# Attention kernel on one Trainium2 core: the sums of the last two batches inverted in other ways, and bias loads, projections and last products in another order

## The chip, the core and the metric

The kernel runs on one core of a Trainium2 chip. The metric is the time of one execution on the device in microseconds (us), as the median of several runs. The core has TensorE (PE in the profile; its weight loads are PEld), VectorE (DVE), ScalarE (ACT), GpSimd (POOL) and SyncE (SP, which here only issues DMAs). All data is 32-bit float.

## What is computed

For 32 images of 256 channels and 32 x 32 positions (S = 1024):

```python
h = group_norm(x, G=32)                       # 8 channels to a group, no scale or shift
q = einsum('oc,bcs->bos', q_w, h) + q_b
k, v = split(einsum('oc,bcs->bos', kv_w, h) + kv_b)
# 8 heads of 32 channels; position s sees positions before it alone
scores = where(strictly_lower, q @ k.T / sqrt(32), -10000)
attn = where(strictly_lower, softmax(scores), 0)
out = x + attn @ v
```

## The kernel before

**Tiles.** An image is a batch of the kernel. Its 8 heads form two groups `g` of four heads (4 x 32 = 128 channels, the partitions). The queries are cut into two halves `hf` of 512. So a batch has four output tiles, n = 2g + hf, each 128 channels x 512 positions.

**Visits.** Scores stand transposed: keys on the partitions (blocks of 128), queries on the free axis. A batch is N = 12 visits, six to a group. In each visit `scores` makes one full piece (4 heads x 512 columns, tile `e`) and one half piece (4 x 256, tile `eh`): score matmuls (L269) into six PSUM banks `sT`, exponentials on ACT (L321 for `e`, L319 for `eh`), and, where a block lies on the diagonal, a mask on POOL (L283). Only blocks that a query can see are made; there is no running maximum. Two of the half piece's matmuls (`first`) stand ahead of the full piece's.

**Loop.** The main loop runs i over all B x N visits and once more. In pass i it issues the scores of visit i, then the functions listed for i under `at`, then `values` of visit i-1, then those under `after`. The order on PE, ACT, DVE and POOL is the order of issue. `when(i, f)` puts a function in such a list; PROJECT, PREPARE, SUMS and FINISH hold the places in visits from the batch's first.

**Values and sums.** `values` multiplies the exponentials with v on TensorE into `acc` (L343). VectorE adds the same exponentials elementwise into the first piece of the tile, `total` (L348), so that the sum over keys in the end needs one reduction over 128 partitions. `num` is ACT's copy of `acc` (L351).

**From total to inverse: three ways.**

- Batches up to B-3 fold: a DMA on POOL's queue adds partitions 64 to 127 of `total` onto 0 to 63, another 32 to 63 onto 0 to 31 (`fold`, L362); SP's DMA stacks the four tiles' 32 rows (`stack`, L368); VectorE turns them in 32 x 32 blocks (L375) and reduces (L376) (`sum_folded`). Then `check_sums` (L434, L435), a reciprocal (L440), a turn (L446), a DMA to DRAM and one back that repeats each head's row over 32 partitions, into `rb` (L453).
- Batch B-2 and the first two tiles of B-1: `sums` multiplies `total` with a matrix of ones on TensorE (`pd`, eight matmuls as counted in the profile, L383), ACT copies the result (`den`, L416), SP writes the rows to DRAM, `gather` reads them back in another shape, and then check, reciprocal and the way over DRAM as above.
- The last two tiles of B-1: `pd` holds the sum on all 32 partitions of a head already, so VectorE takes the reciprocal of the whole 128 x 512 tile in place (`check_here`, `invert_here`, L493). For n = 3 the last three pieces before the final visit, and the final visit's two, are not added by VectorE: `sum_piece` sums them on TensorE.

**Finish.** `finish` is two operations on VectorE (product with the inverse L466; plus v's bias and x L467), a copy of column 0 for tiles with hf = 0 (L469) and a store. `finish_aside` does it with two on POOL (L477, L478) and one on ACT (L479). At the end a count of sums outside a safe range (`outside`) is read by a branch; with the inputs given it goes past the safe version.

**Start.** SP loads x of batch 0 and the weights; ACT's queue loads the three biases. `norm_channels` takes mean and variance per channel on VectorE, two small matmuls (`pm`, `pv`) average over groups, `turn_weights` turns the weights on TensorE, `keep_busy` fills with matmuls on the unit matrix. `projections` gives the 12 units of a batch (8 for q and k, 4 for v) in the order in which they are placed; for batch 0 the first ones run before visit 0.

Of the kernel before, what the change touches and what calls it, by code (L numbers as in the profile page):

```python
# [9 lines left out]
F32 = mybir.dt.float32  # L10
# [21 lines left out]
def tile_norm_attention_residual(  # L32
# [55 lines left out]
    in_range = const.tile([P, ROW + 1], F32, name="in_range")  # L88
# [8 lines left out]
    def unshifted():  # L97
# [24 lines left out]
        def load_weights():  # L122
            for n, w in enumerate((q_w, kv_w[0:C], kv_w[C : 2 * C])):
                live["wn", n] = epool.tile([P, 4, HALFBANK], F32, tag="eh", bufs=4, name=f"wn_{n}")[:, :NG, :C]
                nc.sync.dma_start(out=live["wn", n], in_=w.rearrange("(o p) c -> p o c", p=P))
            nc.scalar.dma_start(out=qk_bias[:, 0, :], in_=q_b.rearrange("(g p) -> p g", p=P))
            nc.scalar.dma_start(out=qk_bias[:, 1, :], in_=kv_b[0:C].rearrange("(g p) -> p g", p=P))
            nc.scalar.dma_start(out=v_bias_col, in_=kv_b[C : 2 * C].rearrange("(g p) -> p g", p=P))
# [112 lines left out]
        def projections(b):  # L241

            qk = [[lambda g=g, hf=hf, n=n: project_qk(b, g, n, hf) for n in range(2)] for g in range(NG) for hf in range(NH)]
            v = [lambda n=n: project_v(b, n) for n in range(NB // 2)]
            return qk[0] + qk[1][:1] + v[:2] + qk[1][1:] + qk[2] + v[2:] + qk[3]
# [29 lines left out]
        def mask(pc, e):  # L275
# [3 lines left out]
            if k < hf * BPH:  # L279
                return  # L280
            n = len(blocks)
            diagonal = e[:, :, : n * P].rearrange("p j (n q) -> p j n q", q=P)
            nc.gpsimd.affine_select(  # L283
                out=diagonal, in_=diagonal, pattern=[[0, 4], [0, n], [1, P]],
                compare_op=ALU.is_gt, fill=0.0, base=0, channel_multiplier=-1,
            )
            if k == 0:
                nc.gpsimd.memset(e[0:1, :, 0:1], 1.0)

        def scores(b, full, half):  # L290
# [8 lines left out]
            first = [scores_of((b, half), short[:, j % 2, 1, :], j) for j in (2, 3)]  # L299


            for n in range(len(full[4])):
                for j in range(4):
                    scores_of((b, full), pairs[j // 2][:, j % 2, :], j, n)

# [22 lines left out]
            mask(full, e)  # L328
# [3 lines left out]
        def values(b, pc, summed=True):  # L332
            g, hf, k, part, blocks = pc
            first, last = k == 0, k == hf * BPH + (1 if hf == 0 else 2)
            e = live.pop(("e", b, pc)) if summed else live["e", b, pc]
# [3 lines left out]
            acc, total = live["acc"], live["sum", b, g, hf]  # L339
            for kb, cols, of in blocks:  # L340
# [6 lines left out]
                if not first and summed:  # L347
                    nc.vector.tensor_add(total[:, :, of], total[:, :, of], e[:, :, cols])  # L348
            if last:
# [38 lines left out]
        def sum_piece(b, pc, start=False, stop=False):  # L388

            if start:  # L390
                live["pd", b] = misc(f"pd_{b}")
            e = live.pop(("e", b, pc))
            for kb, cols, of in pc[4]:
                sum_keys(live["pd", b], e, cols, of, start, stop)

        def sum_total(b):
            sum_keys(
                live["pd", b], live["sum", b, NG - 1, NH - 1], slice(0, HALF), slice(0, HALF), False, False
            )

        def sums(b, g, hf):

            n = NH * g + hf
            den = small.tile([P, HALF], F32, tag="den", name=f"den_{b}_{n}")
            if (b, n) == (B - 1, 3):
                pd = live["pd", b]
            else:
                pd = misc(f"pd_{b}_{n}")
                sum_keys(pd, live.pop(("sum", b, g, hf)), slice(0, HALF), slice(0, HALF))
            if b == B - 1 and n >= 2:  # L410

                most = small.tile([P, 1], F32, tag="most", name=f"most_{n}")
                nc.scalar.activation(den, pd, AF.Identity, accum_out=most)
                live["most", n], live["den", n] = most, pd if n == 3 else den
                return
            nc.scalar.copy(den, pd)  # L416
            if n == 0:
                live["sums", b] = dram.tile([4, 4, HALF], F32, tag="sums", name=f"sums_{b}")
            nc.sync.dma_start(out=live["sums", b][n], in_=den[::HD, :])

        def spread_rows(t):
            return t.rearrange("n j (r c) -> (n j r) c", c=ROW)

        def gather(b, ns):

            if ns.start == 0:
                live["rows", b] = small.tile([P, ROW], F32, tag="rows", name=f"rows_{b}")
            part = slice(ns.start * HD, ns.stop * HD)
            nc.sync.dma_start(out=live["rows", b][part], in_=spread_rows(live["sums", b])[part])

        def check_sums(b, ns):
            part = slice(ns.start * HD, ns.stop * HD)
            rows, ok = live["rows", b][part], in_range[part, :ROW]
# [3 lines left out]
        def invert(b, ns):  # L437
            part = slice(ns.start * HD, ns.stop * HD)
            inv = small.tile([P, ROW], F32, tag="inv", name=f"inv_{b}_{ns.start}")
            nc.vector.reciprocal(inv[part], live["rows", b][part])  # L440
            live["inv", b] = dram.tile([4, 4, HALF], F32, tag="inv", name=f"inverses_{b}_{ns.start}")
            if b >= B - 2:
                nc.sync.dma_start(out=spread_rows(live["inv", b])[part], in_=inv[part])
            else:
                turned = small.tile([P, ROW], F32, tag="inv_turned", name=f"inv_turned_{b}")
                nc.vector.transpose(turned, inv)  # L446
                for n in ns:
                    nc.sync.dma_start(
                        out=live["inv", b][n].rearrange("(a j) (m c) -> (j m) a c", a=2, c=HD),
                        in_=turned[n * HD : (n + 1) * HD].rearrange("p (a c) -> p a c", a=2),  # L450
                    )
            for n in ns:
                nc.sync.dma_start(  # L453
                    out=inverses(b, n),
                    in_=live["inv", b][n].unsqueeze(1).broadcast_to([4, HD, HALF]),
                )

        def inverses(b, n):
            live["rb", b, n] = work.tile([P, HALF], F32, tag="rb", bufs=4, name=f"rb_{b}_{n}")
            return live["rb", b, n]  # L460

# [10 lines left out]
        def finish_aside(b, n, within=slice(0, HALF)):  # L472

            g, hf = divmod(n, NH)
            cols = slice(hf * HALF + within.start, hf * HALF + within.stop)
            num, rb, xt = live["num", b, n], live["rb", b, n][:, within], live["x", b]
            nc.gpsimd.tensor_tensor(rb, num[:, within], rb, ALU.mult)  # L477
# [6 lines left out]
        def check_here(n, ok):  # L484

            least = small.tile([P, 1], F32, tag="least", name=f"least_{n}")
            junk = small.tile([P, HALF], F32, tag="den", name=f"junk_{n}")
            nc.vector.tensor_scalar(junk, live["den", n], SUM_MIN, 1.0, ALU.is_ge, ALU.min, accum_out=least)
            nc.vector.scalar_tensor_tensor(ok, live["most", n], SUM_MAX, least, ALU.is_le, ALU.mult)

        def invert_here(b, n, within):
            rb = live["rb", b, n] if within.start else inverses(b, n)
# [303 lines left out]
```

## Time and profile before

| what | value |
|---|---|
| median of 4 runs | 1836.52 us (1834.83 to 1837.79) |
| profiled execution | 1836.38 us, span 1834.7 us |
| PE busy | 1814.5 us (99%) |
| DVE busy | 1650.2 us (90%) |
| ACT busy | 1481.3 us (81%) |
| POOL busy | 796.2 us (43%) |
| mean granted TensorE clock | 0.996 |

The span runs from the first to the last instruction of the profiled execution; its own time has 1.7 us around it. A row of a timeline gives the start, the length, the engine, the line, the operation, out<-in, shapes, a count, and in brackets how long the engine was idle before it and what ended that. Rows of one line behind each other are merged, so a length can hold several instructions. A row of stretches gives its bounds and length, then busy time by engine (PE, PEld, DVE, ACT, POOL, with counts), the granted clock, the DMA engines' busy share and GB/s.

### The profile page before, as it was taken

How to read it: one execution, taken by the hardware profiler on the slowest of the kernel's cores; microseconds unless marked ns; L12 is line 12 of the kernel's file. 1: busy time of each engine (PE TensorE's matmuls, PEld its weight loads, DVE VectorE, ACT ScalarE, POOL GpSimd, SP SyncE). 2: the span in 40 equal slices, each digit the busy share in tenths (PEclk: the TensorE clock that was granted, in tenths of full speed). 3: DMA queues.
4: the chain of work that ended last, by engine and by line, in shares of the span. 5: the costliest groups of instructions: out<-in, count | busy, mean ns of one | idle time of the engine just before them, and what ended most of it. 6: DMA issues, size and time to landing. Idle time of an engine off the chain costs nothing.

```text
span 1834.7 us, 53874 instructions
## 1 busy us (share of the span) xinstructions
PE 1814.5 (99%) x23200; PEld 925.4 (50%) x23200; DVE 1650.2 (90%) x1747; ACT 1481.3 (81%) x1871; POOL 796.2 (43%) x772
## 2 busy tenths in 40 slices
PE   8999999999999999999999999999999999999997
PEld 5455555555554555554545545555555455455443
DVE  3789999999999999999999999999999999999878
ACT  5888878888788888788887788887888877888775
POOL 1444534435434445444354344454453443444413
PEclk9999999999999999999999999999999999999998
DMA  3447676666766676766666656767667666667412
GB/s 122 70 84 137 138 152 114 127 135 138 145 131 118 134 139 135 152 114 126 136 140 142 133 119 133 140 134 151 116 124 139 137 143 134 120 133 138 87 51 84
DMA packets 77518, 231.46 MB, mean 126 GB/s; under 512 B 20288, under 2 KB 21312, under 8 KB 61912
## 3 DMA queue, kind: packets, MB, share of 16 engines
q0 software_dynamic: 15360, 94.39, 37.3%
q1 hardware_dynamic: 61096, 133.54, 24.1%
q8 instruction: 184, 3.01, 0.7%
q14 instruction: 62, 0.51, 0.1%
q10 hardware_dynamic: 816, 0.00, 0.0%
HBM read 67.42 MB, written 34.64 MB: 56 GB/s over the span
## 4 chain that ended last, share of the span: by engine, by line
PE 94%; DVE 3%; DMA 1%; ACT 1%; issue 0%; SPq 0%; DVEq 0%; ACTq 0%
PE sT L269 30%; PE acc L343 26%; PE pp L156 25%; PE ppv L156 13%; DVE e L348 1%; DMA folded<-e 1%; DVE rb L493 0%; DVE rb L466 0%; DVE rb L467 0%; DMA x<-in_x_dram 0%; ACT e L321 0%; PE pv L156 0%; DMA inverses<-inv_turned 0%; ACT eh L319 0%; PE pd L383 0%
## 5 line engine op out<-in xcount | busy, mean ns | idle before, releaser
L321 ACT ACTIVATE e<-sT 128x1024 f32<-128x1024 f32 x768 | 745.8, 1025 | 273.7 <-PE sT L269 204.7
L348 DVE TENSOR_TENSOR e<-e,e 128x1536 f32<-128x1536 f32 x381 | 638.5, 1676 | 20.3 <-POOL e L283 2.7
L348 DVE TENSOR_TENSOR e<-e,eh 128x1024 f32<-128x1024 f32 x381 | 523.6, 1388 | 132.8 <-PE acc L343 114.5
L283 POOL TENSOR_SCALAR_AFFINE_SELECT e<-e 128x512 f32<-128x512 f32 (+1 forms) x256 | 378.8, 1480 | 592.2 <-ACT e L321 572.1
L269 PE MATMUL sT<-q,k 32*128 32x256 f32 (+3 forms) x7168 | 606.8, 458 | 0.8 <-ACT k L223 0.8
L269 PEld LDWEIGHTS sT<-q,k 32*128 32x128 f32 x7168 | 443.6, 184 | 157.4 <-ACT eh L319 64.4
L156 PE MATMUL pp<-xn,wT 128*32 128x512 f32 x4096 | 492.3, 598 | 0.2 <-ACT den L416 0.2
L343 PE MATMUL acc<-e,v 128*32 128x512 f32 (+2 forms) x4096 | 400.7, 486 | 0.0
L319 ACT ACTIVATE eh<-sT 128x1024 f32<-128x1024 f32 x384 | 397.6, 1035 | 0.0
L362 POOL DMA_DIRECT2D e<-e x240 | 196.6, 825 | 376.6 <-DMA e<-e 286.0
L156 PE MATMUL ppv<-wT,xn 128*32 128x256 f32 x4096 | 247.3, 382 | 0.0
L343 PEld LDWEIGHTS acc<-e,v 128*32 128x32 f32 x4096 | 132.5, 110 | 223.4 <-issue 192.1
L343 PE MATMUL acc<-eh,v 128*32 128x256 f32 x3072 | 224.4, 379 | 0.0
L156 PEld LDWEIGHTS pp<-xn,wT 128*32 128x32 f32 x4096 | 107.0, 109 | 220.1 <-issue 204.3
L343 PEld LDWEIGHTS acc<-eh,v 128*32 128x32 f32 x3072 | 98.4, 110 | 165.0 <-issue 152.9
L156 PEld LDWEIGHTS ppv<-wT,xn 128*32 128x32 f32 x4096 | 120.2, 109 | 102.6 <-issue 29.5
L283 POOL TENSOR_SCALAR_AFFINE_SELECT eh<-eh 128x512 f32<-128x512 f32 x128 | 165.7, 1294 | 0.2
L209 ACT ACTIVATE xn<-x,shift,rstd 128x512 f32<-128x512 f32 x124 | 103.3, 833 | 0.0
L467 DVE SCALAR_TENSOR_TENSOR rb<-rb,v_bias_col,x 128x512 f32<-128x512 f32 x126 | 95.8, 760 | 4.5
L223 ACT ACTIVATE q<-pp,qk_bias 128x512 f32<-128x512 f32 x128 | 91.2, 712 | 1.9 <-PE pp L156 1.9
L223 ACT ACTIVATE k<-pp,qk_bias 128x512 f32<-128x512 f32 x128 | 89.8, 702 | 2.2 <-PE pm L156 1.1
L466 DVE TENSOR_TENSOR rb<-num,rb 128x512 f32<-128x512 f32 x126 | 88.0, 699 | 0.1
(69 smaller groups left out, 669.4 us busy)
## 6 DMA issues: line engine op xcount, KB each, us to landing
e<-e POOLq DMA_DIRECT2D x120, 512.0 KB, 6.3
x<-in_x_dram SPq DMA_DIRECT2D x64, 512.0 KB
out_dram<-rb SPq DMA_DIRECT2D x127, 256.0 KB
rb<-inverses SPq DMA_DIRECT2D x126, 256.0 KB
e<-e POOLq DMA_DIRECT2D x120, 256.0 KB, 4.9
folded<-e SPq DMA_DIRECT2D x120, 256.0 KB
inverses<-inv_turned SPq DMA_DIRECT2D x120, 8.0 KB
wn<-in_L_conv_kv_w_dram SPq DMA_DIRECT2D x2, 256.0 KB
```

The costliest lines, as they stand in the source:

```text
L156: nc.tensor.matmul(out[part], lhsT=lhsT[:, part], rhs=rhs, start=start, stop=stop, skip_group_check=True)
L209: nc.scalar.activation(xn, xt, AF.Identity, bias=live["shift", b][:, g : g + 1], scale=rstd)
L223: nc.scalar.activation(live[key][:, cols], pp, AF.Identity, bias=qk_bias[:, n, g : g + 1], scale=(SCALE, 1.0)[n],)
L269: return nc.tensor.matmul(pair[:, cols], lhsT=live["k", b, g][rows, kb * P : (kb + 1) * P], rhs=live["q", b, g][rows, hf * HALF + of.start ...
L283: nc.gpsimd.affine_select(out=diagonal, in_=diagonal, pattern=[[0, 4], [0, n], [1, P]], compare_op=ALU.is_gt, fill=0.0, base=0, channel_mu ...
L319: exp = nc.scalar.activation(eh.rearrange("p (n bank) q -> p bank n q", n=2), short, AF.Exp)
L321: nc.scalar.activation(e[:, 2 * a : 2 * a + 2, :], pairs[a], AF.Exp)
L343: nc.tensor.matmul(acc[HD * j : HD * (j + 1), of], lhsT=live["v", b][:, kb, h * HD : (h + 1) * HD], rhs=e[:, j, cols], start=first, stop=l ...
L348: nc.vector.tensor_add(total[:, :, of], total[:, :, of], e[:, :, cols])
L362: nc.gpsimd.dma_start(out=total[:rows], in_=total[rows : 2 * rows], accum_op=ALU.add)
L466: nc.vector.tensor_mul(rb, num[:, within], rb)
L467: nc.vector.scalar_tensor_tensor(rb, rb, v_bias_col[:, g : g + 1], xt[:, g, cols], ALU.add, ALU.add)
```

## The change

1. Batch B-2 is folded like the others. Its inverses are made in visit 8 of the last batch (`invert`), tiles 0 and 1 are finished on VectorE in visits 10 and 11, tiles 2 and 3 by `finish_aside` in the closing pass.
2. Each tile of the last batch is summed by `pd` alone and inverted by `invert_here`: VectorE turns the 128 x 512 `den` in 32 x 32 blocks, takes one column of each block (16 columns) for the check and the reciprocal, and turns a repeated reading of them back into the 128 x 512 `rb`. No DRAM is used. Tiles 0 and 1 are finished within the batch; tile 3 is inverted in halves of 256 straight from PSUM, and its `num` stays in `acc`.
3. VectorE adds every piece but those of the final visit; then the sum of tile 3's `total` is made on TensorE behind visit 10's values, and the final visit's pieces are summed ahead of their values.
4. In the final visit the `first` matmuls stand behind the full piece's first block, and the full piece is masked in two pairs of heads.
5. The bias loads go from ACT's queue to SP's, behind the weights; the scaling of q's bias goes behind the first half of batch 0's normalisation.
6. In every batch the first unit of v's projection comes ahead of the third of q and k; for batch 0 it runs before visit 0. The last piece of `norm_apply` comes one visit later.

The core of the diff:

```diff
-            nc.scalar.dma_start(out=qk_bias[:, 0, :], in_=q_b.rearrange("(g p) -> p g", p=P))
+            nc.sync.dma_start(out=qk_bias[:, 0, :], in_=q_b.rearrange("(g p) -> p g", p=P))
...
-            return qk[0] + qk[1][:1] + v[:2] + qk[1][1:] + qk[2] + v[2:] + qk[3]
+            return qk[0] + v[:1] + qk[1][:1] + v[1:2] + qk[1][1:] + qk[2] + v[2:] + qk[3]
...
-            first = [scores_of((b, half), short[:, j % 2, 1, :], j) for j in (2, 3)]
+            last = b == B - 1 and full[:2] == (NG - 1, NH - 1) and half[2] == NB - 2
+            first = [] if last else [scores_of((b, half), short[:, j % 2, 1, :], j) for j in (2, 3)]
...
+                first = first or [scores_of((b, half), short[:, j % 2, 1, :], j) for j in (2, 3)]
...
-            mask(full, e)
+            for heads in (range(2), range(2, 4)) if last else (range(4),):
+                mask(full, e, slice(heads.start, heads.stop))
...
-            if last:
+            if last and (b, g, hf) == (B - 1, NG - 1, NH - 1):
+                live["num", b, NH * g + hf] = acc
+            elif last:
...
+        def sums(b, n):
+            pd = misc(f"pd_{b}_{n}")
+            sum_keys(pd, live.pop(("sum", b, *divmod(n, NH))), slice(0, HALF), slice(0, HALF), True, n < 3)
+            if n == 3:
+                live["den", n] = pd
             else:
+                live["den", n] = small.tile([P, HALF], F32, tag="den", name=f"den_{b}_{n}")
+                nc.scalar.copy(live["den", n], pd)
...
+        def invert_here(b, n, within=slice(0, HALF)):
+            if within.start == 0:
+                inverses(b, n)
+            k = (within.stop - within.start) // HD
+            turned = small.tile([P, HALF], F32, tag="den", name=f"turned_{b}_{n}_{within.start}")[:, : k * HD]
+            nc.vector.transpose(turned, live["den", n][:, within])
+            rows = turned.rearrange("p (k r) -> p k r", r=HD)[:, :, 0]
+            check_sums(rows)
+            inv = small.tile([P, ROW], F32, tag="inv", name=f"inv_{b}_{n}_{within.start}")[:, :k]
+            nc.vector.reciprocal(inv, rows)
+            nc.vector.transpose(
+                live["rb", b, n][:, within].rearrange("p (k r) -> p k r", r=HD),
+                inv.unsqueeze(2).broadcast_to([P, k, HD]),
+            )
...
         def end_last(b):
+            both = [slice(c * HALFBANK, (c + 1) * HALFBANK) for c in range(2)]
+            for part in both:
+                invert_here(b, 3, part)
             worst = const.tile([P, 1], F32, name="worst")
             nc.vector.tensor_reduce(worst, in_range, AX.X, ALU.min)
-            check_here(3, ok)
-            invert_here(b, 3, both[0])
+            pc = misc("pc")
+            nc.tensor.matmul(pc[0:1, 0:1], lhsT=worst, rhs=ones, start=True, stop=True)
+            finish(b, 3, both[1])
+            finish(b, 2)
             outside = const.tile([1, 1], I32, name="outside")
             nc.vector.tensor_scalar(outside, pc[0:1, 0:1], -1.0, float(P), ALU.mult, ALU.add)
-            finish_aside(b, 3, both[0])
-            invert_here(b, 3, both[1])
-            finish(b, 3, both[1])
+            finish(b, 3, both[0])
...
-        PREPARE = (-16, -15, -9, -9, -8, -8, -7, -6, -5, -4)
+        PREPARE = (-16, -15, -9, -9, -8, -8, -7, -6, -5, -3)
...
+                    when(first + N + 8, lambda b=b: invert(b))
...
+                    for n in every[:2]:
+                        when(first + N + 10 + n, lambda b=b, n=n: finish(b, n), after)
+                    for n in every[2:]:
+                        when(first + 2 * N, lambda b=b, n=n: finish_aside(b, n), after)
                 else:
+                    for n in every[:3]:
+                        v = first + SUMS[n]
+                        when(v, lambda b=b, n=n: sums(b, n), after)
+                        v += 1 + n // 2
+                        when(v, lambda b=b, n=n: invert_here(b, n), after)
+                        if n < 2:
+                            when(v, lambda b=b, n=n: finish(b, n), after)
...
+                pcs = products[(i - 1) % N] if i else ()
+                if i == B * N:
+                    for n, pc in enumerate(pcs):
                         sum_piece(B - 1, pc, stop=n == 1)
+                for pc in pcs:
+                    values((i - 1) // N, pc, i < B * N)
                 if i == B * N - 1:
-                    for n, pc in enumerate(products[N - 2] + products[N - 3][1:]):
-                        sum_piece(B - 1, pc, start=n == 0)
+                    sums(B - 1, 3)
```

## The prediction

> **What bounds the kernel now.** I read the page first (engine shares, chain), then the busy time by stretches, then the chain and the timelines of the start and of the last 60 us. Times are from the span's start. TensorE is the chain nearly everywhere:
>
> ```profile
> PE 94%; DVE 3%; DMA 1%; ACT 1%; issue 0%; SPq 0%; DVEq 0%; ACTq 0%
> ```
>
> Stretches from one batch's fourth visit to the next (length, then busy time by engine, last the granted clock and the DMA), and the last one to the end:
>
> ```profile
> 1664.08:1720.07 55.99, 55.99 (x728) 28.59 (x724) 51.94 (x55) 46.08 (x59) 24.27 (x23) 1.00 0.66 133
> 1720.07:1782.40 62.33, 60.63 (x760) 28.91 (x756) 47.26 (x50) 48.32 (x63) 16.90 (x16) 1.00 0.15 46
> 1782.40:1834.70 52.30, 39.12 (x482) 18.41 (x474) 46.13 (x49) 30.64 (x41) 19.77 (x16) 0.90 0.22 80
> ```
>
> A folded batch takes 55.99 us and TensorE never rests in it. The batch whose sums go through TensorE takes 62.33, that is 6.34 more. After 1782.40 VectorE is the full engine (46.13 of 52.30). VectorE's timeline shows where it takes over, and the end:
>
> ```profile
> 1720.07 2.36 DVE L348 TENSOR_TENSOR e<-e,eh 128x1024 f32<-128x1024 f32 x2 [0.70 <-PE acc L343]
> 1782.40 2.36 DVE L348 TENSOR_TENSOR e<-e,eh 128x1024 f32<-128x1024 f32 x2 [1.95 <-PE acc L343]
> 1816.85 1.06 DVE L489 SCALAR_TENSOR_TENSOR in_range<-most,least 128x1 f32<-128x1 f32 x1
> 1817.83 3.34 DVE L493 RECIPROCAL rb<-den 128x512 f32<-128x512 f32 x1
> 1821.20 1.72 DVE L466 TENSOR_TENSOR rb<-num,rb 128x512 f32<-128x512 f32 x1
> 1822.96 1.63 DVE L467 SCALAR_TENSOR_TENSOR rb<-rb,v_bias_col,x 128x512 f32<-128x512 f32 x1
> 1829.54 0.48 DVE L467 SCALAR_TENSOR_TENSOR rb<-rb,v_bias_col,x 128x256 f32<-128x256 f32 x1
> ```
>
> The add at 1782.40 waits for TensorE; from there VectorE runs without a rest to 1830.02. That is 47.62 us; a store and the closing follow to 1834.7. So the end is: when TensorE lets VectorE into visit 3 of the last batch, plus VectorE's own queue. At the start TensorE waits twice, and the load of x dips (DMA busy tenths in steps of 0.5 us):
>
> ```profile
> 8.60 0.24 PE L156 MATMUL pm<-mv,avg 128*32 128x2 f32 x8 [2.48 <-DVE qk_bias L563]
> 17.91 1.57 PE L269 MATMUL sT<-q,k 32*128 32x256 f32 x16 [0.81 <-ACT k L223]
> ...
> DMA  0004878438985999999999999999999971000000
> GB/s 0 0 0 90 238 213 279 140 99 255 410 312 126 288 327 365 395 381 399 434 393 410 401 426 418 393 418 426 401 410 401 418 295 41 0 0 0 0 0 0
> ...
> 5.40:8.70 3.30, 0.82 (x15) 0.66 (x13) 3.00 (x7) 0.00 (x0) 0.00 (x0) 1.00 0.97 308
> 8.80:12.10 3.30, 3.30 (x26) 3.06 (x22) 0.73 (x4) 0.81 (x3) 0.90 (x2) 0.50 1.03 410
> ```
>
> **The last batch but one.** Folding it drops four groups of eight `pd` matmuls (0.86 to 1.06 us each) with the waits beside them: 62.33 - 55.99 = 6.34 us, all on the path. VectorE enters visit 3 at 1782.40 - 6.34 = 1776.06. POOL's fold DMAs and SP's stacks come back as in every other batch.
>
> **VectorE's queue after that.** I take the folded batch 1664.08 to 1720.07 as the template, start to start, and leave out the two things that the last batch has not (deviation 0.86, statistics 1.49 and 1.44). Adds and finish of visit 3: 2.28 + 1.38; adds of visits 4, 5, 6: 3.64 + 4.44 + 4.67; folded sums (L375, L376) 2.67 + 2.79 around the add of visit 7, 1.14; check, reciprocal and turn 1.16; adds of visits 8 to 11: 2.36 + 2.28 + 3.67 + 4.44. Together 36.92; the three adds that the change brings back (L348) are in it.
>
> Each new inversion is a 128x512 turn (0.73 from L375 to L376), two checks of 16 columns (0.20 each, between 0.16 for one column and 0.22 for 64), a reciprocal of 16 (64 columns take 0.54 and 512 take 3.34, so 6.3 ns a column: 0.24, with the gap 0.27) and the turn back, 0.70: 2.10. Three make 6.30. No row turns from a repeated column; it could cost half (0.35) or double (1.40), and I take 0.70, since the rows' turn time goes with the output. Finishing four tiles in the batch costs 2 x 1.58 (with the first column's copy) + 2 x 1.39 = 5.94. At the end: two half inversions 2 x 1.45, the minimum 0.22, two half finishes 2 x 0.94, one whole 1.58, one scalar 0.10 = 6.68. Sum: 36.92 + 6.30 + 5.94 + 6.68 = 55.84, so VectorE ends at 1831.90, against 1830.02: **+1.9 us**. The 6.34 won on TensorE are paid back by 8.2 more on VectorE.
>
> **The port.** VectorE's two-input work lengthens beside POOL: L466 took 0.68 alone and 1.72 at 1821.20 beside POOL's L477; L348 on 1024 columns 1.22 or 1.94. The template holds 2.4 us of this (visits 5, 6, 11). In the new order VectorE meets some masks in turns, and the turn took 0.70 with POOL at work too (1737.30), so between 0 and 2.4 goes: **-1.2**. Against it, both `finish_aside` of the last batch but one now stand on POOL behind the last masks (four products of 1.27 to 1.59) beside the last adds: by the row above one costs VectorE 1.0; none to four can, 0 to +4.2: **+1.0**, as most of VectorE's last 10 us are turns and small pieces. The Trainium skill, "SBUF — State Buffer", section "SBUF: two separate sides", says the pair of ports is an exclusive lock that a two-input VectorE operation or a GpSimd one holds whole. By that rule all four could block VectorE in turn; the sum would be some 3 us higher.
>
> **Waits the change adds.** (a) The third sum of the last group: `pd` of n=3 now waits on VectorE's adds of visit 11's turn, with the last `pd` pieces and values queued behind it. By the sum these adds end 10.2 before VectorE's end (1.39 + 2.10 + 6.68), while TensorE, whose visits without a projection take 3 to 4.5 us, is there some 7 us earlier, so it stands idle. In the start's rows a stretch with 0.82 busy of 3.30 is followed by one at clock 0.50, and so is the idle end of the span. The Trainium skill, "TensorE: Matmul & The Clock Gate", Part 1, says the same of an idle window of about 3.4 us. At half clock the 0.9 + 1.5 us of `pd` become 4.8; VectorE has 3.5 of other work (a finish and an inversion) meanwhile: **+1.3** (0 to 2.4). (b) ACT's copy of `den` for n=1 takes a buffer that `sum_folded` in front of it is using, so exponentials wait behind it, some 4 us; before, the same copy (1743.69) stood 2.18 behind L376. VectorE then has 1.4 + 1.16 + 2.36 + 2.10 + 1.39 = 8.4 us queued before the adds of the visit behind it; ACT and TensorE need 0.59 for the copy, 2.75 for the exponentials, 1.50 for the next scores and 0.86 for the values, 5.7: hidden with 2.7 to spare, and only what goes over 8.4 would show. (c) `rb` of the last batch waits for stores of two visits earlier, landed by then. SP's round trip for the inverses (3.2 + 1 us at 1746.23) starts two visits before the first finish that needs it: hidden.
>
> **The start.** The value projection fills the 0.81 idle at 17.91: -0.75, kept, since TensorE then is the chain up to visit 3 of the last batch. The three bias loads (816 packets for 3 KB) go behind x and the weights on SP. The rate falls to 140 and 99 GB/s while they run, between 279 and 255; without the dip the first half of x lands about 1.1 earlier (0 to 1.8): **-1.1**. The Trainium skill, "DMA: Bandwidth & Descriptors", section "Issuing engines are not separate DMA queues", says another issuing engine saves only issue time; by that the sum is 1.1 higher. With x earlier the idle stretch ahead of 8.60 shortens, and the 3.3 us at clock 0.50 behind it may not come: 0 to 1.2, **-0.6**. Moving the scaling of the bias: 0 to -0.05. All: -2.5.
>
> **Inside each batch** one value projection and one query projection change places, and one normalisation moves a visit: TensorE has the same instructions, ACT 9.9 us free of 55.99; nothing. The last visit's split masks and order: two selects of 0.68 for one of 1.10, under wait (a); nothing.
>
> **Sum.** 1.9 - 1.2 + 1.0 + 1.3 - 2.5 = +0.5. The profiled execution took 1836.38 (span 1834.7), 0.14 below the median of the four runs, 1836.52. Forecast 1837.0: within 0.2% (3.7 us), which is about what a measurement of this kernel can tell from no change.
>
> **Rivals.** Faster: the tolls do not come. VectorE meets no masks (-2.4), the asides fall on turns (0), the clock holds (0), the start gives 2.5 to 3.8: 1.9 - 2.4 - 2.5 (or 3.8) = -3.0 to -4.3, and with turns back at half (-1.4) to -5.7; the middle is 1832.1. For it: TensorE's side is 6.34 earlier for certain. Against: VectorE is full in every stretch. Slower: the port. All four POOL products hit VectorE (+4.2) and the template keeps its 2.4: 1.9 + 4.2 + 1.3 - 2.5 = +4.9, 1841.4. It decides once the products cost over 3.0 with the template whole. For it: the row at 1821.20; against: one-input work pays nothing. That the start does nothing but fill the idle 0.81 is a third: +0.5 + 1.7 = +2.2, 1838.7, still within 0.2%.
>
> **Numbers.** Forecast 0.38, start without effect 0.09 (both the same), faster 0.30, slower 0.23. The likeliest case's own range is 1832.9 to 1840.2. 1831.5 to 1841.5 leaves about 0.1 on each side.
>
> **To be seen afterwards.** Visit 3's add some 6.3 + 2.5 earlier and still waiting on TensorE; no gap of VectorE from there to the end, some 55 us; inversions of 2.1; a clock of 0.5 ahead of the last values; x landing before 4.5. Wrong it is if VectorE has gaps in the last batch, if the turn back is far from 0.70, or if a folded batch no longer takes 56.0.

## The result, and the profile after

The kernel after takes 1839.13 us (median of 38 runs, 1837.91 to 1841.76), the kernel before 1836.83 (58 runs, 1834.72 to 1838.60). The ratio is 1.0015 with a 95% interval of 1.0010 to 1.0019: 2.3 us more, inside the 0.2% that the prediction calls no change, and resolved as a small loss by this many runs. The profiled execution took 1839.42, span 1837.6, against 1836.38 and 1834.7.

The page's chain of work is still TensorE's, and the busy time by stretches (columns as before) shows both ends of the trade. The first two rows are two batches, the last one runs from VectorE's entry into the last batch's visit 3 to the end:

```profile
PE 97%; DVE 2%; issue 0%; ACT 0%; DMA 0%; DVEq 0%; ACTq 0%
```

```profile
1660.76:1716.75 55.99, 55.99 (x728) 28.58 (x724) 51.92 (x55) 46.14 (x59) 25.08 (x24) 1.00 0.67 134
1716.75:1772.74 55.99, 55.99 (x728) 28.59 (x724) 49.93 (x49) 46.13 (x59) 22.73 (x23) 1.00 0.63 116
1772.74:1837.60 64.86, 41.48 (x458) 19.18 (x450) 57.71 (x76) 28.88 (x36) 23.10 (x15) 0.87 0.19 63
```

The batch that took 62.33 now takes 55.99, as forecast. The last stretch grew from 52.30 to 64.86, with VectorE 57.71 busy. VectorE's timeline shows its entry and the rows that grew (in this kernel the add of `values` is L353, a finish L464 and L465, a check L413 and L414, a turn L450 and back L455; the experiments' numbers differ by one or a few):

```profile
1772.74 2.36 DVE L353 TENSOR_TENSOR e<-e,eh 128x1024 f32<-128x1024 f32 x2 [0.70 <-PE acc L347]
...
1815.86 2.58 DVE L353 TENSOR_TENSOR e<-e,e 128x2048 f32<-128x2048 f32 x1
1818.54 2.10 DVE L353 TENSOR_TENSOR e<-e,eh 128x1024 f32<-128x1024 f32 x1
1820.57 1.76 DVE L464 TENSOR_TENSOR rb<-num,rb 128x512 f32<-128x512 f32 x1
1822.36 1.64 DVE L465 SCALAR_TENSOR_TENSOR rb<-rb,v_bias_col,x 128x512 f32<-128x512 f32 x1
1823.92 0.70 DVE L450 STREAM_TRANSPOSE turned<-den 128x512 f32<-128x512 f32 x1
1824.66 0.51 DVE L413 SCALAR_TENSOR_TENSOR in_range<-turned,in_range 128x16 f32<-128x16 f32 x1
1825.20 0.18 DVE L414 SCALAR_TENSOR_TENSOR in_range<-turned,in_range 128x16 f32<-128x16 f32 x1
...
1831.98 0.48 DVE L465 SCALAR_TENSOR_TENSOR rb_last<-rb_last,v_bias_col,x 128x256 f32<-128x256 f32 x1
```

VectorE enters visit 3 at 1772.74 instead of 1782.40, 9.66 earlier, still waiting for TensorE; then it works without a gap to 1832.46, 59.72 us instead of 47.62. What follows its end takes 5.14 instead of 4.68. So the span changes by -9.66 + 12.10 + 0.46 = +2.90. The turns take 0.70 as alone, but the finish of 0.69 + 0.75 took 3.4 (L464 and L465, 1820.57 to 1823.92) and the first of two equal checks 0.51 instead of 0.18. POOL's timeline in the same place:

```profile
1816.28 3.28 POOL L475 TENSOR_TENSOR rb<-num,rb 128x512 f32<-128x512 f32 x1
1819.64 2.13 POOL L476 TENSOR_TENSOR rb<-rb,x 128x512 f32<-128x512 f32 x1
1821.73 1.72 POOL L475 TENSOR_TENSOR rb<-num,rb 128x512 f32<-128x512 f32 x1
1823.53 1.60 POOL L476 TENSOR_TENSOR rb<-rb,x 128x512 f32<-128x512 f32 x1
```

These are the two products and the two additions of `finish_aside` (the four products of the prediction), each 1.27 to 1.29 beside VectorE's reciprocal in the kernel before. They and VectorE's two-input work lengthen each other, and the rows show how: each waits until the other engine's row under way has ended, and then takes its own time alone. VectorE's add at 1818.54 has POOL's product beside it until 1819.56 and takes 1.22 alone; that makes 1820.78, and it ended at 1820.64. All eight such rows here, from POOL's product at 1816.28 to VectorE's check at 1824.66, end 0.13 to 0.20 ahead of this sum. The turn at 1823.92, with one input, does not wait.

At the start, TensorE's timeline, the two stretches shown before, and the DMA rows of the first 20 us:

```profile
7.61 0.24 PE L156 MATMUL pm<-mv,avg 128*32 128x2 f32 x8 [1.50 <-DVE mv L167]
...
16.48 1.57 PE L269 MATMUL sT<-q,k 32*128 32x256 f32 x16
```

```profile
5.40:8.70 3.30, 1.80 (x21) 1.45 (x19) 2.48 (x8) 0.17 (x1) 0.00 (x0) 1.00 0.69 209
8.80:12.10 3.30, 3.29 (x38) 2.52 (x42) 1.83 (x5) 1.83 (x4) 0.90 (x2) 1.00 1.04 408
```

```profile
DMA  0006598999989973159999999999999981000000
GB/s 0 0 0 82 188 336 287 393 434 358 301 283 358 363 244 44 1 85 427 410 410 434 434 410 410 410 442 426 410 426 377 385 344 41 25 25 0 0 0 0
```

The dip to 140 and 99 GB/s is gone, `pm` starts 1.0 earlier, the wait of 0.81 before the first scores is gone, and the stretch behind the rest ran at clock 1.00 instead of 0.50. The first values start at 26.57 instead of 29.72: 3.15 earlier, and 3.15 + 6.34 are 9.49 of the 9.66.

### The profile page after: what moved, and what is told of

Its sections match the earlier page's. It is cut to its first block, busy times and chain, and to the rows that moved or that the text cites. A ratio compares the mean times of both kernels' runs of the same rounds, so it can differ in the third digit from the quotient of the medians.

```text
span 1837.6 us, 53791 instructions
## 1 busy us (share of the span) xinstructions
PE 1810.6 (99%) x23144; PEld 924.4 (50%) x23144; DVE 1664.2 (91%) x1774; ACT 1479.5 (81%) x1862; POOL 805.7 (44%) x779
## 4 chain that ended last, share of the span: by engine, by line
PE 97%; DVE 2%; issue 0%; ACT 0%; DMA 0%; DVEq 0%; ACTq 0%
PE sT L269 31%; PE acc L347 26%; PE pp L156 26%; PE ppv L156 13%; DVE e L353 1%; DVE rb L465 0%; DMA x<-in_x_dram 0%; DVE rb L464 0%; PE pv L156 0%; ACT e L324 0%; DVE st L166 0%; DVE turned L382 0%; DVE turned L450 0%; PE pm L156 0%; DVE rb_last L465 0%
## 5 line engine op out<-in xcount | busy, mean ns | idle before, releaser
L353 DVE TENSOR_TENSOR e<-e,e 128x1536 f32<-128x1536 f32 x382 | 642.3, 1681 | 17.9
L353 DVE TENSOR_TENSOR e<-e,eh 128x1024 f32<-128x1024 f32 x383 | 528.7, 1394 | 124.5 <-PE acc L347 102.6
L369 POOL DMA_DIRECT2D e<-e x248 | 203.1, 825 | 391.1 <-DMA e<-e 297.9
L465 DVE SCALAR_TENSOR_TENSOR rb<-rb,v_bias_col,x 128x512 f32<-128x512 f32 x123 | 94.3, 767 | 4.4
L383 DVE TENSOR_REDUCE rows<-turned 128x16 f32<-128x512 f32 x124 | 85.0, 686 | 4.3
```

The source lines that it names most:

```text
L369: nc.gpsimd.dma_start(out=total[:rows], in_=total[rows : 2 * rows], accum_op=ALU.add)
L383: nc.vector.tensor_reduce(live["rows", b][:, j * HALF // HD : (j + 1) * HALF // HD], turned.rearrange("p (k r) -> p k r", r=HD), AX.X, ALU ...
L465: nc.vector.scalar_tensor_tensor(rb, rb, v_bias_col[:, g : g + 1], xt[:, g, cols], ALU.add, ALU.add)
```

## The experiments

Each kernel had 10 or 11 runs beside 32 or 33 runs of the kernel before, whose median was 1836.70 to 1836.74 in all three sets. Theory: what the start and TensorE give, VectorE's longer queue takes back, and the part of it that the prediction missed is the port that VectorE and POOL share. Rivals: the time went into the new waits, or folding itself costs more than it saves.

**The start.** Parts 5 and 6 of the change alone, on the kernel before; then the bias loads and their scaling alone:

```diff
-            nc.scalar.dma_start(out=qk_bias[:, 0, :], ...)      # all three biases
+            nc.sync.dma_start(out=qk_bias[:, 0, :], ...)
...
-            return qk[0] + qk[1][:1] + v[:2] + ...              # first alone
+            return qk[0] + v[:1] + qk[1][:1] + v[1:2] + ...
```

> The kernel before with the start's part alone: bias loads on SP behind the weights, the scaling of q's bias later, the value projection ahead of visit 0, and the places that go with it. In the two profiles the first values of batch 0 stand at 29.72 (before) and 26.57 (after), 3.15 us earlier. Theory (TensorE is the chain up to the last batch, so the start's gain is kept to the end, and the rest of the change loses 5.5 us in the last batch): 3.1 us faster than before, 1833.7, with the add of the last batch's visit 3 at 1779.3 in place of 1782.40. Rival (what the start wins is given back inside the batches or at VectorE's queue in the last batch): 0 to 1 us faster. Folded batches stay at 55.99 us by the theory.

> The kernel before with the bias loads on SP behind the weights and the scaling of q's bias behind the first half of the normalisation; projections stay in their old order. Theory (the loads of 4 bytes hold up x, and x 0.9 us earlier also ends the idle stretch before the clock falls to 0.50): x lands near 4.5, clock 1.00 between 8.8 and 12.1, first projection near 11.2 in place of 13.46, 2.3 us faster than before, with the 0.81 us wait ahead of the first scores still there. Rival (another queue saves only issue time): 0 to 0.1 us, with x at 5.4.

The start alone: 1834.19 (ratio 0.9985, 0.9976 to 0.9994), 2.55 less (3.1 expected). The bias part alone: 1835.38 (0.9989, 0.9980 to 0.9998), 1.36 less (2.3 expected), with the wait of 0.82 for `k` still there. By the medians parts 5 and 6 are worth what was forecast, 2.5, so the rest of the change costs 1839.13 - 1834.19 = 4.9. Not all of the 2.5 arises at the start: in the profiled execution the first values come 1.48 earlier (28.24) and visit 3's add 2.24 earlier, and 0.59 of this arises in the last batch but one, which takes 61.74 instead of 62.33 (1718.42 to 1780.16). The whole change folds that batch, so the 0.59 is no part of what it gains at its start. With the start alone VectorE enters visit 3 at 1780.16 and its queue is 47.64 (before 47.62): the start doesn't touch the end. In both profiles the stretch 8.80 to 12.10 ran at clock 0.63 and 0.65, though the first of these starts had 1.00 in the kernel after. Three kernels below that have the start of the kernel after unchanged had 0.52 (asides held), 1.00 (three pieces back) and 0.62 (fill-in ahead of the third sum). So the clock there differs between executions. The next run keeps TensorE from resting there:

```diff
-            keep_busy(11)
+            keep_busy(15)      # on the kernel after
```

> The kernel after, with 15 fill-in matmuls in place of 11 at the start, so that TensorE does not rest ahead of the first mean. Theory (the clock of the stretch behind that rest differs from execution to execution, and this is what spreads the times): the clock in 8.8 to 12.1 is 1.00, the slow group of times about 1840.5 to 1841.5 is gone, median 1838.9 to 1838.0, spread under 2 us. Rival (the spread comes from elsewhere): median 1839.1 and the same spread of almost 4 us.

The stretch 8.80 to 12.10 in two executions with the same loads, first the one of the run on wait (a) below (11 fill-in matmuls), then this one (15):

```profile
8.80:12.10 3.30, 3.30 (x26) 3.06 (x26) 1.47 (x5) 1.61 (x4) 0.91 (x2) 0.62 1.02 417
```

```profile
8.80:12.10 3.30, 3.19 (x35) 2.51 (x38) 1.69 (x6) 1.83 (x4) 0.91 (x2) 1.00 1.01 415
```

Measured 1839.28 (1838.27 to 1839.94). The kernel after has 12 of 38 times above 1840.3, this one none of 11. That fits an upper group of executions whose clock fell at the start; the clock of this stretch is known for the profiled executions alone. All six with 15 fill-in matmuls had 1.00 in this stretch; of the six with 11 and the bias loads on SP, two had 1.00 and four 0.52 to 0.65. The median didn't move (forecast 1838.0 to 1838.9), because by their times most executions of the kernel after have the full clock already. The Trainium skill, "TensorE: Matmul & The Clock Gate", Part 1, says the window over which activity is judged runs freely and doesn't start with the kernel; a rest of 1.59 us followed by 1.00 in one execution (three pieces back) and one of 1.42 followed by 0.52 in another (asides held) agree with that.

**Folding alone.** The last batch but one folded, on the kernel before; its four tiles finished on VectorE in visits 10 and 11 of the last batch:

```diff
-                first, last, late = b * N, b == B - 1, b >= B - 2
+                first, last, late = b * N, b == B - 1, b == B - 1
...
-                        when(first + FINISH[late][n], lambda b=b, n=n: finish(b, n), after)
+                        when(first + (FINISH[0][n] if b < B - 2 else N + 10 + n // 2), lambda b=b, n=n: finish(b, n), after)
```

> The kernel before, with the last batch but one folded as the others and nothing else of the change: its four tiles are finished on VectorE in visits 10 and 11 of the last batch, and the last batch keeps its own sums and its way over DRAM. Theory (VectorE's queue sets the end): VectorE enters visit 3 at 1776.1, 6.3 earlier, but carries 5.5 more of turns and reductions from there, so it ends 0.5 to 1 earlier: 1835.7 to 1836.4, and with tolls at the port up to 1838. Rival (what TensorE saves comes off the time): 1830.5.

(The inverses of the last batch take the buffer of the folded sums, which is free by then.) 1837.56 (ratio 1.0003, 0.9994 to 1.0012): nothing gained, as in the theory's case with tolls. VectorE's timeline:

```profile
1777.21 2.36 DVE L348 TENSOR_TENSOR e<-e,eh 128x1024 f32<-128x1024 f32 x2 [0.70 <-PE acc L343]
...
1805.75 0.22 DVE L434 SCALAR_TENSOR_TENSOR in_range<-rows,in_range 64x64 f32<-64x64 f32 x1 [1.54 <-DMA rows<-sums]
...
1831.09 0.48 DVE L472 SCALAR_TENSOR_TENSOR rb_last<-rb_last,v_bias_col,x 128x256 f32<-128x256 f32 x1
```

The entry is 5.19 earlier than before (6.34 less 1.18 that this execution lost at its start, first scores at 19.09 instead of 17.91). Its stretches read clock 1.00 there, but its fill-in matmuls took 421 ns each up to 14.3, as in the kernel before at clock 0.50, and not the 275 ns of that kernel from 12.7 on: the durations show a dip that the clock column misses. The queue is 54.36, 6.7 longer, of which 5.5 are the turns and reductions and 1.5 the wait for the sums' way over DRAM. The rival in which TensorE's 6.3 come off the time falls.

**The port.** First, the asides held until VectorE's last finish in the batch is done; POOL starts with a one-column product that reads its result:

```diff
+            if n == 2:
+                held = small.tile([P, 1], F32, tag="held", name="held")
+                done = live["rb", b, 1][:, 0:1]
+                nc.gpsimd.tensor_tensor(held, done, done, ALU.mult)
```

> The changed kernel with one small POOL product ahead of the asides that reads the finished tile 1 of the last batch but one, so that the four POOL products start only when VectorE begins the inversion of tile 2. Theory (POOL's products lengthen VectorE's two-input work: 2.26 for 1.58, 3.35 for 1.39 and 4.71 for 4.44 in the queue of after): visit 11's adds and the finish behind them go back to 4.4 and 1.4, the six checks of the inversions may each pay some tenths, VectorE ends 1.5 to 2.5 us earlier, 1837.0. Rival one (the late sums at half clock set the end): no gain, VectorE waits for TensorE instead. Rival two (the lock of the ports is paid wherever the products stand): the checks and the last finishes take the 2.5 us, 1839 as after.

1839.21 (ratio 1.0009, 1.0000 to 1.0018): no change. VectorE's rows:

```profile
1821.37 0.69 DVE L464 TENSOR_TENSOR rb<-num,rb 128x512 f32<-128x512 f32 x1
1822.09 0.75 DVE L465 SCALAR_TENSOR_TENSOR rb<-rb,v_bias_col,x 128x512 f32<-128x512 f32 x1
...
1823.49 0.88 DVE L413 SCALAR_TENSOR_TENSOR in_range<-turned,in_range 128x16 f32<-128x16 f32 x1
...
1826.03 0.97 DVE L413 SCALAR_TENSOR_TENSOR in_range<-turned,in_range 128x8 f32<-128x8 f32 x1
```

The finish is back at 1.4, but two checks of 16 and 8 columns now pay 0.70 and 0.80. The queue is 58.28, 1.44 shorter than after; but this execution entered visit 3 1.65 later (1774.39), so the time settles nothing. Leaving POOL's work out is the cleaner test. Both kernels have the 15 fill-in matmuls, so 1839.28 is their base; first the four products of `finish_aside` go (two output tiles lack the inverse and x), then the last batch's masks from its eighth visit on as well:

```diff
-            nc.gpsimd.tensor_tensor(rb, live["num", b, n], rb, ALU.mult)
-            nc.gpsimd.tensor_tensor(rb, rb, xt[:, g, cols], ALU.add)
-            nc.scalar.activation(rb, rb, AF.Identity, bias=v_bias_col[:, g : g + 1])
+            nc.scalar.activation(rb, live["num", b, n], AF.Identity, bias=v_bias_col[:, g : g + 1])
...
-            if k < hf * BPH:
+            if k < hf * BPH or live.get("bare"):      # second kernel only
```

> The kernel after with 15 fill-in matmuls at the start, with POOL's four products of finish_aside left out: ACT writes the values plus bias alone, so two output tiles lack the inverse and x. Theory (VectorE's last finish and checks are long because of POOL): about 2.3 less on VectorE (0.9 in the finish, 1.35 in the checks); then the sums at half clock are late by 0.5: 1837.5. Rival (no toll of the port, these operations are long for another reason): 1839.3.

> As the one before, and the masks of the last batch from its eighth visit on are left out too, so POOL does nothing beside VectorE's last 30 us; sums and values there include keys that should be masked. Theory (the port is the excess of VectorE's queue over the forecast): another 1.4 less on VectorE, of which the wait for the sums at half clock takes back 0.5: 1836.6, VectorE's queue from visit 3 about 56.5 in place of 59.5. Rival (the queue is long without POOL): 1839.3 and 59.5.

1837.34 (1.94 less) and 1835.28 (another 2.06 less; ratio to the kernel before 0.9991, 0.9982 to 1.0000). VectorE's timeline of the second:

```profile
1773.07 2.36 DVE L354 TENSOR_TENSOR e<-e,eh 128x1024 f32<-128x1024 f32 x2 [0.70 <-PE acc L348]
...
1779.12 1.51 DVE L354 TENSOR_TENSOR e<-e,eh 128x1024 f32<-128x1024 f32 x1
...
1783.36 1.48 DVE L466 SCALAR_TENSOR_TENSOR rb<-rb,v_bias_col,x 128x512 f32<-128x512 f32 x1
...
1784.94 2.58 DVE L354 TENSOR_TENSOR e<-e,e 128x2048 f32<-128x2048 f32 x1
1787.62 1.51 DVE L354 TENSOR_TENSOR e<-e,eh 128x1024 f32<-128x1024 f32 x1
1789.24 2.77 DVE L354 TENSOR_TENSOR e<-e,e 128x1536 f32<-128x1536 f32 x2
...
1816.82 1.23 DVE L354 TENSOR_TENSOR e<-e,eh 128x1024 f32<-128x1024 f32 x1
1817.96 0.69 DVE L465 TENSOR_TENSOR rb<-num,rb 128x512 f32<-128x512 f32 x1
1818.68 0.75 DVE L466 SCALAR_TENSOR_TENSOR rb<-rb,v_bias_col,x 128x512 f32<-128x512 f32 x1
...
1820.09 0.18 DVE L414 SCALAR_TENSOR_TENSOR in_range<-turned,in_range 128x16 f32<-128x16 f32 x1
...
1821.99 0.45 DVE L451 STREAM_TRANSPOSE turned<-pd 128x256 f32<-128x256 f32 x1 [0.60 <-PE pd L391]
...
1827.80 0.48 DVE L466 SCALAR_TENSOR_TENSOR rb_last<-rb_last,v_bias_col,x 128x256 f32<-128x256 f32 x1
```

The same instructions in the same order, 2.10 + 1.76 + 1.64 in the kernel after, are 1.23 + 0.69 + 0.75 with POOL empty. VectorE's queue is 59.46 in the base, 57.39 without asides, 55.21 without masks too. None of the three is toll and own work alone: a gap of 0.46 stands in the base, and waits for `pd` of 0.72 and 0.60 in the other two. The base's row, and the one without asides:

```profile
1808.37 2.36 DVE L353 TENSOR_TENSOR e<-e,eh 128x1024 f32<-128x1024 f32 x2 [0.46 <-PE acc L347]
```

```profile
1824.56 0.45 DVE L450 STREAM_TRANSPOSE turned<-pd 128x256 f32<-128x256 f32 x1 [0.72 <-PE pd L390]
```

Without them the queues are 59.00, 56.67 and 54.61, so the asides cost VectorE 2.3 in the base, as expected, and the late masks 2.1, where 1.4 were expected. In the kernel after, whose queue of 59.72 has no gap and whose last masks lie beside the same rows as in the run without asides, the asides cost 59.72 - 56.67 = 3.05. The rival (long for another reason) falls. The early masks, which the second run keeps, still lengthen the five rows from 1779.12 to 1789.24: alone such rows took 1.23, 0.75, 2.29, 1.23 and 2.44, so an estimate of the early masks' toll is 1.9.

**The waits.** Wait (a), TensorE idle before the third sum: 40 fill-in matmuls in that place.

```diff
+                    keep_busy(40)
                     sums(B - 1, 3)
```

> The kernel after, with 40 matmuls on the unit matrix ahead of the third sum of the last group, so that TensorE does not rest before it. Theory (the wait on the third sum is hidden behind VectorE's finish and inversion, which the port has lengthened): pd runs at the full clock and some 2 us shorter, VectorE ends where it did, time 1839.1 within 0.7. Rival (the term of +1.3 in the prediction stands in the time): 1837.8 or less.

1839.24, no change, but the test is poor. TensorE's timeline in the kernel after, then in this one, then VectorE's in this one:

```profile
1820.70 3.64 PE L390 MATMUL pd<-e,pick 128*32 128x512 f32 x24 [6.55 <-DVE e L353]
1824.11 0.85 PE L390 MATMUL pd<-eh,pick 128*32 128x256 f32 x8
```

```profile
1817.63 9.20 PE L142 MATMUL busy<-ident 128*128 128x128 f32 x80
1826.76 1.93 PE L390 MATMUL pd<-e,pick 128*32 128x512 f32 x24
```

```profile
1829.18 0.45 DVE L450 STREAM_TRANSPOSE turned<-pd 128x256 f32<-128x256 f32 x1 [1.89 <-PE pd L390]
```

`pd` ran in 1.93 instead of 3.64, but the fill lasted until 5.5 after VectorE's adds were done and made VectorE wait 1.89. This execution, at 1841.93, is the second slowest of the eleven, and its clock fell at the start too, so the 1.89 may not stand in the median. In the kernel after, `pd` and its second row are over at 1824.96 and VectorE asks at 1826.21, so nothing is lost there. The 0.72 and 0.60 above are the price once the port's toll no longer covers it. Wait (b), ACT's copy behind `sum_folded`: a buffer of its own for it, on the base with 15 fill-in matmuls.

```diff
-                live["den", n] = small.tile([P, HALF], F32, tag="den", ...)
+                pool = (work, "num", 8) if n == 1 else (small, "den", 2)
+                live["den", n] = pool[0].tile([P, HALF], F32, tag=pool[1], bufs=pool[2], ...)
```

> The kernel after with 15 fill-in matmuls at the start (1839.28), and the sum of the last batch's tile 1 copied into a buffer of its own, so that ACT's copy no longer waits for sum_folded. Theory (that wait is nearly hidden): ACT's idle 7.5 and TensorE's 2.15 ahead of the projection shrink below 2, TensorE does not fall to half clock in 1796 to 1804, VectorE loses only its gap of 0.46 in visit 9: 1838.8. Rival (the wait is what the change lost): 1837.0 or less.

ACT's row for this copy in the kernel after, and in this one:

```profile
1799.05 0.58 ACT L409 COPY den<-pd 128x512 f32<-128x512 f32 x1 [7.52 <-DVE rows L383]
```

```profile
1794.84 0.59 ACT L410 COPY den<-pd 128x512 f32<-128x512 f32 x1 [3.45 <-PE pd L390]
```

The wait is gone and the time is 1839.99, 0.7 more than 1839.28: both theories miss. VectorE no longer has its gap of 0.46 in visit 9, but TensorE, ACT and POOL come to the last masks earlier, and VectorE's rows are longer there: its queue is 60.45, against 59.46 with the gap. (The two profiled executions took the same, 1839.38 and 1839.40, so the 0.7 rests on the medians.) Two of this kernel's rows, which in the base were 2.54 and 1.47:

```profile
1816.20 3.16 DVE L353 TENSOR_TENSOR e<-e,e 128x2048 f32<-128x2048 f32 x1
1819.47 2.10 DVE L353 TENSOR_TENSOR e<-e,eh 128x1024 f32<-128x1024 f32 x1
```

**Versions that beat both.** VectorE is the engine that ends last, and TensorE stands idle 6.55 before `pd`. So the last three pieces go back to TensorE, as in the kernel before, with the rest of the change kept; then 15 fill-in matmuls are added; then the own buffer as well:

```diff
-                for pc in pcs:
-                    values((i - 1) // N, pc, i < B * N)
+                for n, pc in enumerate(pcs):
+                    values((i - 1) // N, pc, i < B * N - 2 or (i == B * N - 2 and n == 0))
                 if i == B * N - 1:
                     sums(B - 1, 3)
+                    for pc in products[N - 2] + products[N - 3][1:]:
+                        sum_piece(B - 1, pc)
```

> The changed kernel with one part undone: the last three pieces ahead of the final visit are summed on TensorE again, behind tile 3's total, and not added by VectorE. Theory (VectorE's queue sets the end, TensorE stands idle 6.55 us there): VectorE loses three adds, 2.39 + 2.10 + 1.44 = 5.9 us, TensorE gains about 1.8 us of matmuls inside its idle time; VectorE's end 5 to 6 us earlier, or 3 to 4 if the masks and pieces of the final visit become what it waits for; 1833.5 to 1835. Rival (the end hangs on the final visit's exponentials, masks and pd): VectorE gets a gap of the same length ahead of the last inversion, within 1 us of after, 1838.5 to 1839.

> Both: the last three pieces summed on TensorE as in the kernel before, and 15 fill-in matmuls at the start. Theory: 1832.8 to 1833.6, since 1832.82 was the profiled time of the version without the extra matmuls in an execution with the clock at 1.00, and its median was 1834.56. Rival (the clock at the start is not what spreads the times): 1834.6.

> The version with the last three pieces summed on TensorE and 15 fill-in matmuls (1832.70), and a buffer of its own for the sum of tile 1. Theory: VectorE has no gap there, so 1832.5 within 0.5. Rival: masks come earlier and meet other work of VectorE, 1834.

1834.56 (ratio to before 0.9987, 0.9978 to 0.9996), 1832.70 (0.9977, 0.9968 to 0.9987) and 1833.77 (0.9982, 0.9973 to 0.9991). The second is the best: 4.0 below the kernel before. VectorE's queue from visit 3 is 53.03 in the first and `pd` needs no wait; the fill-in matmuls give 1.9, since 7 of 11 times of the first lie above 1834 and one of 10 of the second. TensorE's `pd` in the second, now at full clock and without idle before it:

```profile
1814.09 1.90 PE L390 MATMUL pd<-e,pick 128*32 128x512 f32 x16
```

The own buffer costs 1.1 here (VectorE's queue is 54.12) as it cost 0.7 above, and the rival (earlier masks meet other work) holds.

## Why the prediction came out as it did

1839.13 is within 0.2% of before and inside the range, as forecast; the point was 2.1 too low. Term by term, on the profiled executions, with VectorE's queue split into its own work and the port's toll (the template's 2.4 of toll taken out of 55.84):

| term of the prediction | forecast | shown |
|---|---|---|
| last batch but one folded | -6.34 | -6.34 (55.99) |
| start | -2.5 | -3.15 in the execution with the full clock; -2.55 by the medians of the start alone |
| VectorE's queue, own work | 53.4 | some 52.7 (54.61 less the early masks' estimated 1.9) |
| port, in all | 2.2 (2.4 - 1.2 + 1.0) | some 7.0 (early masks 1.9, late masks 2.1, asides 3.05) |
| wait (a) | +1.3 | 0 after; 0.72 and 0.60 with the asides' toll gone |
| wait (b) | 0 | 0 after; gaps of 0.46 and 0.51 in two other executions, and taking the wait away costs 0.7 |
| close behind VectorE | 0 | +0.46 |

**What held.** The mechanism: TensorE's saving is certain and VectorE's queue pays it back. Folding alone gains nothing, and in the profiled execution VectorE never rests from its entry to its end. The price of a turn from a repeated column, for which the trace had no row, was 0.71 against 0.70 taken, and a whole inversion 2.07 against 2.10.

**What failed** is the size of the port term. The prediction assumed that the last masks would meet turns and took 1.2 off the template, and that one of four products would hit two-input work. In the kernel after, the masks of the last visits still fell on adds and finishes, and the products on an add, a finish and a check: 3.05, just over the 3.0 that the slower rival named as its deciding point, and near the case in which all four block VectorE in turn, which the prediction names and does not take. That rival's mechanism was right, with 6.6 of toll in its sum. Its 1841.4 was too high mainly because wait (a) was not paid and VectorE entered earlier. The rival of a start without effect came nearest in the number, 1838.7, but parts 5 and 6 alone gained 2.55, so its condition did not hold.

**What cancelled.** The queue was 59.72 against 55.6 + 1.3 = 56.9: 2.8 more, that is 4.8 of toll less 1.3 of wait and 0.7 of own work. VectorE's entry came 9.66 earlier against 8.84, 0.8 more, and the close took 0.46: 2.8 - 0.8 + 0.5 = 2.5, which is what the profiled executions' +3.04 exceeds the forecast's +0.5 by. So wait (a) and the port are not independent terms: a long toll covers the wait, and a short one leaves 0.6 to 0.7 of it. That the point was only 2.1 off, with the toll missed by more than twice that, is partly luck.

## What to carry to other kernels

When a change moves work from an engine that ends early to the one that ends last, the time it saves elsewhere is only lent: price it on the last engine's queue from the point at which that engine takes over. Toll between VectorE and POOL is not a constant to subtract: lay the two queues side by side, let a two-input row and POOL's row take turns, bound the toll by the whole of POOL's work in the stretch, and test it by leaving that work out. A wait covered by such a toll comes back when the toll goes, so take both away together, or move work to the idle engine, which is what won here.

## What the runs showed of the hardware

VectorE's longest check, and POOL's product beside it, in the kernel after with 15 fill-in matmuls:

```profile
1824.42 1.20 DVE L414 SCALAR_TENSOR_TENSOR in_range<-turned,in_range 128x16 f32<-128x16 f32 x1
```

```profile
1824.32 1.27 POOL L475 TENSOR_TENSOR rb<-num,rb 128x512 f32<-128x512 f32 x1
```

- A check of 16 or 8 columns on VectorE, 0.17 to 0.18 alone, took up to 1.20 beside POOL's product of 1.27, so a tiny instruction can pay for a whole neighbour. The Trainium skill, "SBUF — State Buffer", section "SBUF: two separate sides", says the loser of the shared pair of ports is blocked for the other's whole instruction; these checks agree. The long adds and products agree too, if each is given what was left of the neighbour's row: the add of 2048 columns, 2.29 alone, took 2.54, 2.58 or 3.16 where POOL's row had 0.40, 0.44 or 1.01 left, and POOL's product of 1.27 took 3.28 where VectorE's add had 2.16 left.
- Turns and reductions do not lengthen: over the whole kernel after, 124 turns of 128x512 took 701 ns in the mean and 124 reductions 686, while POOL was busy 44% of the span.
- The three bias loads (3 KB) held back the load of x when they ran beside it from another queue: behind x and the weights on x's queue the first statistics start at 4.54 (4.68 with the start alone, 4.80 with the bias part alone) instead of 5.42.
- A rest of TensorE of 1.2 to 1.8 us at the start was followed by clock 1.00 in some executions and 0.52 to 0.65 in others. With the start alone, at 0.63, the first values came at 28.24, in the kernel after, at 1.00, at 26.57.
